# Holding back the fronts of the first six images, and image 0's second normalization in double steps

## The chip, the cores and the metric

The kernel runs on one core of a Trainium2 chip. The metric is the device time of one execution in microseconds (us). The kernel before was timed three times: the median is 1356.12 us, the lowest 1348.22 and the highest 1360.93.

## The reference

The input x has 32 images of 256 channels and 32 x 32 pixels in fp32. Two layers follow one another; each normalizes its input in groups of 8 channels (over all pixels of an image) and adds its result to what it got.

```python
x = x + conv3x3(quantize(gn(x)), quantize(w)) quantized, + bias          # layer 0
x = x + involution7x7(gn(x))                                             # layer 1

def involution(x):
    y = relu(bn(w1 @ x))                  # 256 -> 64 channels, per pixel
    w = w2 @ y + b2                       # 16 groups x 49 taps, per pixel
    out[c, p] = sum over taps of w[group(c), tap, p] * x[c, p + tap]
```

The quantization rounds to half precision. So layer 0 is an ordinary convolution whose weights are shared by all images. Layer 1 has weights of its own for every pixel, worked out from the normalized image, and every pixel's sum needs 49 of them for each of 16 groups.

## The kernel before, in words

**One image's path.** The generator `front(b)` (line 284) does what comes ahead of the window sums. Its statistics go over both halves of 128 channels: `add_up` (line 211) sums by a ScalarE activation with an accumulator, `group` (line 218) adds over 8 channels by two VectorE transposes and a reduction, `means`, `squares`, `variances`, `scales` and `finish` (lines 233 to 267) give 1/sigma (`rstd`) and the offset (`off`). `apply` (line 269) writes the normalized fp16 image `xq`. The convolution has four units (two halves of the pixels by two halves of the output channels). Each is 18 matmuls of 128x512 in two batches of nine (line 332); its PSUM result `pc` goes by way of `q` (line 346) back into x (line 348), and ScalarE sums x again (line 352). For image 0, every second unit uses another PSUM buffer, so two units can follow each other at once; else there is one buffer, and the next unit waits for `q`. Then the second normalization: mean, squares, variance, finish, and `xn` in two halves of channels, each with the left and the right side of the pixels (line 370). From `xn` come the features `py` and `y` (lines 377 and 388), and by transposes `pt` the `pixels` (lines 396 and 400).

**Weights and bands.** `weights(b, r0)` (line 403) makes `pw` from `y` with 32 small matmuls for four rows of pixels, eight times an image, and `evict` (line 435) writes them on VectorE into the ring `w_sb`. `scatter` (line 465) sends them by SP's queue to a DRAM buffer `wd`, seven transfers for each of four row blocks k of an image; `load_bands` (line 478) brings the block back as a band matrix, 14 transfers by POOL's queue and two by SP's. There are three band buffers. `sums` (line 510) multiplies band and pixels on TensorE into `acc`, `add_windows` (line 530) adds this to x, and `store` sends it out.

**The order.** It is written out by hand: the loop at line 556 counts a stage n, with 16 stages for each image. Every engine executes its instructions in exactly this order. Stages of image b, before: its front begins at n = 16b - 56 and takes some 50 stages, one step in each, so three or four fronts run at once; `weights` begins at 16b - 18, the sums at 16b. In every stage the fronts' steps come first, then the sums, then the weights. A front's steps, counted from its begin: statistics in steps 0 to 8, convolution from step 9 (a batch of nine matmuls in every second step) to 26, second normalization from 27 to 35, `py` at 36, transposes from 42.

```python
            later = list(fronts)
            for part in range(2):
                for b in list(later):
                    got = next(fronts[b], fronts)
```

A front that yields `LATER` goes on in the same stage, after the others have had their step.

Ahead of the first convolution VectorE writes the weights `wq` from a staging area that lies in two of the band buffers (`quantize_weights`, line 193); POOL clears these buffers and `w_sb` afterwards.

Of the kernel before, what the change touches and what calls it, by code (L numbers as in the profile page):

```python
# [9 lines left out]
F32 = mybir.dt.float32  # L10
AF = mybir.ActivationFunctionType
ALU = mybir.AluOpType

P = 128
B, C, H, W = 32, 256, 32, 32
N = H * W
NT = 512
RT = NT // W
CH = C // P
# [6 lines left out]
GN = 8  # L26
SQ = 32
GN_EPS = 1e-5
# [44 lines left out]
FRONT = -56  # L73
LOAD = -63
LEAD = 18


@with_exitstack
def tile_quant_conv_then_involution(
# [10 lines left out]
    nc = tc.nc  # L90
# [4 lines left out]
    small = ctx.enter_context(tc.tile_pool(name="small", bufs=2))  # L95
# [5 lines left out]
    ps_m = ctx.enter_context(tc.tile_pool(name="ps_m", bufs=1, space=PSUM))  # L101
# [40 lines left out]
    bands = [const.tile([P, SIDES, WINC * WB + PAD], F32, name=f"band_{i}") for i in range(NBAND)]  # L142
# [11 lines left out]
    wq = const.tile([P, CH, K0 * K0, C], F16, name="wq")  # L154
# [26 lines left out]
    for col, cols, at, n in (  # L181
# [4 lines left out]
        to = bass.AP(  # L186
            tensor=wd.tensor,
            offset=wd.offset + col * WPIX + at,
            ap=[[ROW, H], [WPIX, cols], [1, n]],
        )  # L190
        nc.sync.dma_start(to, bands[NBAND - 1][:H, 0, :n].unsqueeze(1).to_broadcast([H, cols, n]))

    def quantize_weights(kh):

        nc.vector.tensor_scalar(wq[:, kh], staged[kh], F16_MAX, -F16_MAX, ALU.min, ALU.max)
        nc.gpsimd.memset(bands[kh], 0.0)
        if kh == CH - 1:
            nc.gpsimd.memset(w_sb, 0.0)

    class GroupNorm:  # L200


        def __init__(self, b, layer):
            self.tiles = list(sums_sb[b % 2][layer])

        def begin(self, parts):
# [4 lines left out]
        def add_up(self, src, part, h, n0, n1, func, bias=0.0):  # L211
            junk = work.tile([P, N], F16, tag="junk", name="junk", bufs=1)
            i = part * CH + h
            nc.scalar.activation(  # L214
                junk[:, n0:n1], src[:, h, n0:n1], func, bias=bias, accum_out=self.sums[:, i : i + 1]
            )

        def group(self):


            if self.parts == 2:
                nc.vector.tensor_add(self.sums[:, :CH], self.sums[:, :CH], self.sums[:, CH : 2 * CH])
            across = small.tile([P, SQ], F32, tag="across", name="across")
            nc.vector.transpose(across, self.sums)  # L224
            total = small.tile([P, SQ // GN], F32, tag="total", name="total")
            nc.vector.tensor_reduce(
                total, across.rearrange("p (g r) -> p g r", r=GN), mybir.AxisListType.X, ALU.add
            )
            back = small.tile([P, SQ], F32, tag="back", name="back")
            nc.vector.transpose(back, total.unsqueeze(2).to_broadcast([P, SQ // GN, GN]))  # L230
            return back[:, :CH]
# [10 lines left out]
        def variances(self):  # L242
            pv = self.group()
            self.s = small.tile([P, CH], F32, tag="s", name="s")
            nc.scalar.activation(self.s, pv, AF.Sqrt, bias=eps, scale=1.0 / (GN * N))  # L245
            self.ve = small.tile([P, CH], F32, tag="ve", name="ve")
            nc.scalar.activation(self.ve, pv, AF.Identity, bias=eps, scale=1.0 / (GN * N))

        def scales(self):
# [3 lines left out]
        def finish(self):  # L253

            t = small.tile([P, CH], F32, tag="t", name="t")
            nc.scalar.activation(t, self.r, AF.Square)
            w = small.tile([P, CH], F32, tag="w", name="w")
            for h in range(CH):
                nc.scalar.mul(w[:, h : h + 1], t[:, h : h + 1], self.ve[:, h : h + 1])
            u = small.tile([P, CH], F32, tag="u", name="u")  # L260
            nc.scalar.activation(u, w, AF.Identity, bias=three_halves, scale=-0.5)
            self.rstd = small.tile([P, CH], F32, tag="rstd", name="rstd")
            self.off = small.tile([P, CH], F32, tag="off", name="off")
            for h in range(CH):
                one = slice(h, h + 1)
                nc.scalar.mul(self.rstd[:, one], u[:, one], self.r[:, one])
                nc.scalar.mul(self.off[:, one], self.m[:, one], self.rstd[:, one])
# [7 lines left out]
    LATER = 1  # L275

    def backwards(at):

        step, n = at.ap[-1]
        return bass.AP(tensor=at.tensor, offset=at.offset + step * (n - 1), ap=[*at.ap[:-1], [-step, n]])  # L280
# [3 lines left out]
    def front(b):  # L284


        xt = x_tiles[b]

        def stages(n):
            for _ in range(n):  # L290
                yield

        gn = GroupNorm(b, 0)
        gn.begin(1)
        for h in range(CH):
            gn.add_up(xt, 0, h, 0, N, AF.Identity)
            yield
        yield LATER
        gn.means()
# [12 lines left out]
        gn = GroupNorm(b, 1)  # L312
        gn.begin(N // NT)
        units = [(nt, mh) for nt in range(N // NT) for mh in range(CH)]
        for s in range(4 * len(units) + 2):
            u, i = divmod(s, 4)
            if u < len(units):
                nt, mh = units[u]
                if i == 0 and b == 0 and u % 2:

                    pc = ps_m.tile([P, NT], F32, tag="m", name="pc")
                elif i == 0:
                    pc = ps_c.tile([P, NT], F32, tag="pc", name="pc")
                for n in range(sum(CONV[:i]), sum(CONV[: i + 1])):
# [3 lines left out]
                    kh, k = n // (K0 * K0), (k + K0 * K0 // 2) % (K0 * K0)  # L328
# [7 lines left out]
                        start=n == 0,  # L336
                        stop=n == CH * K0 * K0 - 1,
# [28 lines left out]
        for h in range(CH):  # L366
            yield
            to = xn[:, h].rearrange("p (k d r j) -> p d k r j", d=SIDES, r=TR, j=JC)
            at = xt[:, h].rearrange("p (k r d j) -> p d k r j", d=SIDES, r=TR, j=JC)
            gn.apply(h, [(to[:, 0], at[:, 0]), (to[:, 1], backwards(at[:, 1]))])  # L370
        yield from stages(2)

        py = ps_m.tile([P, NT], F32, tag="m", name="py")
        for kh in range(CH):
            px = xn[:, kh].rearrange("p (a i n) -> p a i n", i=2, n=2 * JC)
            for i in range(2):
# [4 lines left out]
                    start=kh == 0,  # L381
                    stop=kh == CH - 1,
                )
        to = y_sb[b % 2].rearrange("p (k r d j) -> p d k r j", k=K, d=SIDES, j=JC)
        of = py.rearrange("p (k d r j) -> p d k r j", k=K, d=SIDES, j=JC)
        for d in range(SIDES):
            at = of[:, d]
# [3 lines left out]
        for m in range(0, M, 2):  # L391
# [7 lines left out]
            to = pixels[(b * M + m) // 2 % NPIX].rearrange("p i a (v c) -> p (i a) v c", c=GC)  # L399
# [130 lines left out]
    def add_windows(b, m):  # L530

        d = m % SIDES
        to = x_tiles[b].rearrange("p h (r c) -> p h r c", c=W)
        j0 = d * (JC - PAD1)
        for g, at, top, f, l in windows(b, m):
            x_at = to[:, :, f:l, j0 : j0 + WINI]
            of = at.rearrange("p h j r -> p h r j")[:, :, f - top : l - top]
            nc.vector.tensor_tensor(x_at, of, x_at, ALU.add)  # L538

    def store(b, k):  # L540

        cols = slice(k * NT, (k + 1) * NT)
        nc.sync.dma_start(out[b].rearrange("(h p) n -> p h n", p=P)[:, :, cols], x_tiles[b][:, :, cols])
# [3 lines left out]
    per = 2 * M  # L547

    def due(n, lag):

        b, i = divmod(n - lag, per)
        return (b, i) if 0 <= b < B else (None, None)

    with tc.manual_schedule():
        fronts = {}
        for n in range(FRONT, B * per + 2):
            b, i = due(n, FRONT)
            if i == 0:
                fronts[b] = front(b)
            later = list(fronts)  # L560
            for part in range(2):
                for b in list(later):
                    got = next(fronts[b], fronts)
                    if got is fronts:
                        fronts.pop(b)
                    if got is not LATER:
                        later.remove(b)
            if n in (FRONT + CH, FRONT + CH + 4):
                quantize_weights((n - FRONT - CH) // 4)
            b, i = due(n, 0)  # L570
            if b is not None and i % 2 == 0:
                sums(b, i // 2)
            b, i = due(n, 1)
            if b is not None and i % 2 == 0:
                add_windows(b, i // 2)
                if i // 2 == M - 1:
                    store(b, 1)
                    x_tiles.pop(b)

            b, i = due(n, 2)  # L580
            if b is not None and i == 2 * (M - 1 - SIDES):
                store(b, 0)
            b, i = due(n, -LEAD)
            if b is not None and i % 2 == 0:
                weights(b, i // 2 * WR)

            for part in range(2):
                b, i = due(n, -LEAD + 1 + part)
                if b is not None and i % 2 == 0:
                    for k in range(K):  # L590
                        if i // 2 == min((k + 1) * TR // WR, H // WR - 1):
                            scatter(b, k, part)
            b, i = due(n, LOAD)
            if i == 0 and b > 1:
                x_tiles[b] = load_x(b)

            b, i = due(n, 3 - 4 * NBAND)
            if b is not None and i % 4 == 0:
                load_bands(b, i // 4)
# [38 lines left out]
```

## Time and profile before

| | |
|---|---|
| median of three timed runs | 1356.12 us |
| the profiled execution | 1344.24 us |
| its span | 1342.5 us |
| TensorE busy | 1253.6 us (93%), mean granted clock 0.982 |
| VectorE, ScalarE, POOL busy | 61%, 55%, 76% |
| DMA | 361.85 MB, mean 270 GB/s |

The span is the time from the first to the last instruction of one execution under the hardware profiler; all starts in the timeline count from its begin. "Busy" counts the time in which an engine has an instruction at work. For TensorE the ends of the matmuls are modelled. In the answers PE is TensorE's matmuls, PEld its weight loads, DVE VectorE, ACT ScalarE; a name ending in q is an engine's queue as it issues transfers. A row of the timeline has its start and length in us, engine, line, operation, what it writes and reads, the shape, how many instructions it merges, and in brackets how long the engine had been idle and what released it. A row of the waits has the waiting engine and line, whom it waited for, the us in total, how often, and the longest.

### The profile page before, as it was taken

How to read it: one execution, taken by the hardware profiler on the slowest of the kernel's cores; microseconds unless marked ns; L12 is line 12 of the kernel's file. 1: busy time of each engine (PE TensorE's matmuls, PEld its weight loads, DVE VectorE, ACT ScalarE, POOL GpSimd, SP SyncE). 2: the span in 40 equal slices, each digit the busy share in tenths (PEclk: the TensorE clock that was granted, in tenths of full speed). 3: DMA queues.
4: the chain of work that ended last, by engine and by line, in shares of the span. 5: the costliest groups of instructions: out<-in, count | busy, mean ns of one | idle time of the engine just before them, and what ended most of it. 6: DMA issues, size and time to landing. Idle time of an engine off the chain costs nothing.

```text
span 1342.5 us, 65799 instructions
## 1 busy us (share of the span) xinstructions
PE 1253.6 (93%) x27648; PEld 763.7 (57%) x27648; DVE 818.8 (61%) x2539; ACT 733.3 (55%) x1731; POOL 1014.4 (76%) x1818
## 2 busy tenths in 40 slices
PE   5899999999999999999999999999999999999665
PEld 2356566565555655556655556666555566556454
DVE  3466666565666665656665666766666666666442
ACT  5775656455656556556545655655556564553300
POOL 9067878777787778777778787788777877788785
PEclk9999999999999999999999999999999999999987
DMA  6089999999999999999999999999999999999995
GB/s 228 11 237 295 271 293 293 279 266 281 272 286 282 291 285 270 283 263 280 293 282 283 270 288 282 293 297 296 281 288 275 277 284 290 271 281 266 278 274 166
DMA packets 360724, 361.85 MB, mean 270 GB/s; under 512 B 75056, under 2 KB 304752, under 8 KB 359152
## 3 DMA queue, kind: packets, MB, share of 16 engines
q1 hardware_dynamic: 278512, 229.38, 56.8%
q0 software_dynamic: 81920, 128.28, 33.9%
q8 instruction: 220, 3.60, 1.1%
q14 instruction: 72, 0.59, 0.1%
HBM read 176.60 MB, written 180.76 MB: 266 GB/s over the span
## 4 chain that ended last, share of the span: by engine, by line
PE 60%; DMA 23%; POOL 7%; issue 3%; ACT 3%; DVE 2%; SPq 1%; POOLq 0%; DVEq 0%; ACTq 0%
PE pc L332 25%; PE acc L522 19%; DMA band<-wd 17%; PE pw L411 11%; POOL band L497 7%; DMA wd<-w_sb 6%; PE pt L396 3%; PE py L377 3%; ACT junk L214 1%; SPq L476 1%; DVE w_sb L435 1%; DMA x<-in_x 1%; ACT xn L273 0%; SPq L497 0%; ACT xq L273 0%
## 5 line engine op out<-in xcount | busy, mean ns | idle before, releaser
L497 POOL DMA_DIRECT2D band<-wd x1792 | 980.3, 549 | 315.7 <-DMA band<-wd 182.0
L435 DVE TENSOR_TENSOR w_sb<-pw,late_sb 128x224 f32<-128x224 f32 (+7 forms) x1280 | 330.4, 322 | 419.5 <-PE pw L411 419.2
L332 PE MATMUL pc<-xq,wq 128*128 128x496 f16 (+3 forms) x2304 | 535.2, 379 | 20.3 <-ACT xq L273 18.3
L522 PE MATMUL acc<-band,pixels 64*32 64x190 f32 (+1 forms) x16384 | 426.6, 332 | 51.8 <-DMA band<-wd 42.7
L522 PEld LDWEIGHTS acc<-band,pixels 64*32 64x32 f32 x16384 | 304.7, 107 | 159.7 <-issue 81.1
L332 PEld LDWEIGHTS <-wq 128*128 128x128 f16 x2304 | 206.7, 98 | 316.1 <-issue 102.7
L411 PE MATMUL pw<-late_sb,y 64*32 64x224 f32 (+1 forms) x8192 | 288.9, 333 | 10.8 <-issue 9.4
L538 DVE TENSOR_TENSOR x<-acc,x 128x380 f32<-128x380 f32 (+1 forms) x512 | 262.0, 512 | 32.2 <-PE acc L522 23.2
L411 PEld LDWEIGHTS pw<-late_sb,y 64*32 64x32 f32 x8192 | 186.5, 106 | 38.1 <-issue 21.0
L400 ACT COPY pixels<-pt 128x512 f32<-128x512 f32 x128 | 73.7, 576 | 228.6 <-PE pt L396 228.6
L214 ACT ACTIVATE junk<-x 128x512 f16<-128x512 f32 (+1 forms) x192 | 146.4, 763 | 14.7 <-DVE x L348 12.2
L214 ACT ACTIVATE junk<-x,mean 128x1024 f16<-128x1024 f32 x128 | 147.1, 1149 | 4.3
L245 ACT ACTIVATE s<-back,eps 128x2 f32<-128x2 f32 x64 | 18.9, 296 | 178.6 <-DVE back L230 178.6
L346 DVE TENSOR_SCALAR q<-pc 128x512 f16<-128x512 f32 x128 | 87.2, 681 | 17.6 <-PE pc L332 17.6
L273 ACT ACTIVATE xn<-x,off,rstd 128x512 f32<-128x512 f32 x128 | 96.2, 800 | 0.0
L348 DVE SCALAR_TENSOR_TENSOR x<-q,early_sb,x 128x512 f32<-128x512 f16 x128 | 94.2, 736 | 0.3
L396 PEld LDWEIGHTS pt<-ident,xn 128*128 128x128 f32 x512 | 63.9, 142 | 26.3 <-issue 2.5
L396 PE MATMUL pt<-ident,xn 128*128 128x128 f32 x512 | 78.0, 275 | 0.1
L273 ACT ACTIVATE xq<-x,off,rstd 128x1024 f16<-128x1024 f32 x64 | 75.7, 1227 | 0.0
L235 ACT ACTIVATE mean<-back 128x2 f32<-128x2 f32 x64 | 12.6, 196 | 101.4 <-DVE back L230 101.4
L377 PE MATMUL py<-xn,early_sb 128*64 128x512 f32 x256 | 62.2, 606 | 0.9 <-ACT xn L273 0.9
L224 DVE STREAM_TRANSPOSE across<-sums 128x32 f32<-128x32 f32 x128 | 26.3, 205 | 33.6 <-ACT junk L214 32.4
(40 smaller groups left out, 369.3 us busy)
## 6 DMA issues: line engine op xcount, KB each, us to landing
wd<-w_sb SPq DMA_DIRECT2D x896, 160.0 KB
band<-wd POOLq DMA_DIRECT2D x1664, 70.5 KB, 4.6
x<-in_x SPq DMA_DIRECT2D x64, 512.0 KB
out<-x SPq DMA_DIRECT2D x64, 512.0 KB
band<-wd POOLq DMA_DIRECT2D x128, 60.5 KB, 4.6
band<-wd SPq DMA_DIRECT2D x128, 50.5 KB
band<-wd SPq DMA_DIRECT2D x128, 40.5 KB
band<-in_w SPq DMA_DIRECT2D x2, 1152.0 KB
```

Source lines behind the costliest of these rows:

```text
L214: nc.scalar.activation(junk[:, n0:n1], src[:, h, n0:n1], func, bias=bias, accum_out=self.sums[:, i : i + 1])
L273: nc.scalar.activation(dst, src, AF.Identity, bias=self.off[:, one], scale=self.rstd[:, one])
L332: nc.tensor.matmul(pc.rearrange("p (r c) -> p r c", c=W)[:, r0 - nt * RT : r1 - nt * RT, c0:c1], wq[:, kh, k, mh * P : (mh + 1) * P], xq[: ...
L346: nc.vector.tensor_scalar(q, pc, F16_MAX, -F16_MAX, ALU.min, ALU.max)
L348: nc.vector.scalar_tensor_tensor(xt[:, mh, cols], q, bias_sb[:, mh : mh + 1], xt[:, mh, cols], ALU.add, ALU.add)
L377: nc.tensor.matmul(py[i * CR : (i + 1) * CR], w1_sb[:, kh, :], px[:, :, i], start=kh == 0, stop=kh == CH - 1,)
L396: nc.tensor.transpose(pt[:, i, h * P : (h + 1) * P], xn[:, h, (m + i) * P : (m + i + 1) * P], ident)
L411: nc.tensor.matmul(pws[i][t * TW : (t + 1) * TW, : dj.stop - dj.start, r], y_sb[b % 2][half, (r0 // 2 + r) * W : (r0 // 2 + r + 1) * W], w ...
L435: nc.vector.tensor_tensor(to, of[:, :, d0:d1], bias[:, :, d0:d1], ALU.add)
L497: queue.dma_start(to, src)
L522: nc.tensor.matmul(at[t * TW : (t + 1) * TW, h, :, f - top : l - top], px[p, a, v * GC : v * GC + TW], of[:, :, a, f - top : l - top, v], ...
L538: nc.vector.tensor_tensor(x_at, of, x_at, ALU.add)
```

## The change

1. The fronts of images 0 to 5 are held back by 5, 5, 4, 3, 2 and 1 stages at their begin (`HELD`). They catch up later: in the last stages before their stage 37, as many as they were held, each takes two steps instead of one. So image 0 takes its steps 27 to 36, the second normalization and the features, in five double stages, while image 1, which has been held as long, is five steps less far than before in any stage until it catches up itself.
2. For image 0 the sum of the second half of channels goes to VectorE, the finish of both its normalizations to five VectorE operations, and one side of each half of `xn` to VectorE.
3. The clearing of the two staging buffers comes after both halves of `wq` are written, and the second half is written one stage later.
4. Ten matmuls on `wq` whose result nothing reads stand before the first convolution (`warm_up`).

```diff
+WARM = 10
+HELD = {0: 5, 1: 5, 2: 4, 3: 3, 4: 2, 5: 1}
+CATCH = 37
...
-        nc.gpsimd.memset(bands[kh], 0.0)
         if kh == CH - 1:
+            for t in bands[:CH]:
+                nc.gpsimd.memset(t, 0.0)
             nc.gpsimd.memset(w_sb, 0.0)
+    def warm_up():
+
+        pc = ps_m.tile([P, NT], F32, tag="m", name="warm_pc")
+        for _ in range(WARM):
+            nc.tensor.matmul(pc, wq[:, 0, 0, :P], wq[:, 0, 1:3], start=True, stop=True)
...
+        def add_up_by_vector(self, src, h):
+            nc.vector.tensor_reduce(self.sums[:, h : h + 1], src[:, h], mybir.AxisListType.X, ALU.add)
...
+            if self.first:
+                nc.vector.tensor_scalar(self.ve, pv, 1.0 / (GN * N), GN_EPS, ALU.mult, ALU.add)
+                return
...
+            if self.first:
+                self.rstd = small.tile([P, CH], F32, tag="rstd", name="rstd")
+                self.off = small.tile([P, CH], F32, tag="off", name="off")
+                nc.vector.tensor_mul(t, self.r, self.r)
+                nc.vector.tensor_mul(t, t, self.ve)
+                nc.vector.tensor_scalar(t, t, -0.5, 1.5, ALU.mult, ALU.add)
+                nc.vector.tensor_mul(self.rstd, t, self.r)
+                nc.vector.tensor_mul(self.off, self.m, self.rstd)
+                return
...
-            gn.add_up(xt, 0, h, 0, N, AF.Identity)
+            if b == 0 and h:
+                gn.add_up_by_vector(xt, h)
+            else:
+                gn.add_up(xt, 0, h, 0, N, AF.Identity)
...
-            gn.apply(h, [(to[:, 0], at[:, 0]), (to[:, 1], backwards(at[:, 1]))])
+            if b == 0:
+                one = slice(h, h + 1)
+                nc.vector.tensor_scalar(
+                    to[:, 0], at[:, 0], gn.rstd[:, one], gn.off[:, one], ALU.mult, ALU.add
+                )
+            else:
+                gn.apply(h, [(to[:, 0], at[:, 0])])
+            gn.apply(h, [(to[:, 1], backwards(at[:, 1]))])
...
-            later = list(fronts)
-            for part in range(2):
-                for b in list(later):
...
-            if n in (FRONT + CH, FRONT + CH + 4):
-                quantize_weights((n - FRONT - CH) // 4)
+            steps = [[b for b in fronts if not 0 <= n - FRONT - b * per < HELD.get(b, 0)]]
+            for b, held in HELD.items():
+                if CATCH - held <= n - FRONT - b * per < CATCH:
+                    steps.append([b])
+            for later in steps:
+                for part in range(2):
+                    for b in list(later):
+                        got = next(fronts[b], fronts)
...
+            if n == FRONT + HELD[0] + CH:
+                quantize_weights(0)
+                warm_up()
+            if n == FRONT + HELD[0] + CH + 5:
+                quantize_weights(1)
```

More of the change, by code (lines that the diff above doesn't have):

```diff
@@ L195, in quantize_weights @@
         nc.vector.tensor_scalar(wq[:, kh], staged[kh], F16_MAX, -F16_MAX, ALU.min, ALU.max)
-        nc.gpsimd.memset(bands[kh], 0.0)
         if kh == CH - 1:
+            for t in bands[:CH]:
+                nc.gpsimd.memset(t, 0.0)
             nc.gpsimd.memset(w_sb, 0.0)
+    def warm_up():
+        pc = ps_m.tile([P, NT], F32, tag="m", name="warm_pc")
+        for _ in range(WARM):
+            nc.tensor.matmul(pc, wq[:, 0, 0, :P], wq[:, 0, 1:3], start=True, stop=True)
     class GroupNorm:
         def __init__(self, b, layer):
+            self.first = b == 0
             self.tiles = list(sums_sb[b % 2][layer])
@@ L559, in tile_quant_conv_then_involution @@
                 fronts[b] = front(b)
-            later = list(fronts)
-            for part in range(2):
-                for b in list(later):
[L563 to L567, printed above, removed]
-            if n in (FRONT + CH, FRONT + CH + 4):
-                quantize_weights((n - FRONT - CH) // 4)
+            steps = [[b for b in fronts if not 0 <= n - FRONT - b * per < HELD.get(b, 0)]]
[6 more added lines that the diff above has]
+                        got = next(fronts[b], fronts)
+                        if got is fronts:
+                            fronts.pop(b)
+                        if got is not LATER:
+                            later.remove(b)
+            if n == FRONT + HELD[0] + CH:
[3 more added lines that the diff above has]
+                quantize_weights(1)
             b, i = due(n, 0)
```

## The prediction

> **What bounds the kernel now.** I read the page's totals first, then a table of stages, then the start in order of time, then the waits of the transfer queues.
>
> ```profile
> PE 1253.6 (93%) x27648; PEld 763.7 (57%) x27648; DVE 818.8 (61%) x2539; ACT 733.3 (55%) x1731; POOL 1014.4 (76%) x1818
> ...
> DMA  6089999999999999999999999999999999999995
> ```
>
> TensorE and the DMA engines are both near full from the third slice on. The stages (columns: stretch, its length, busy us of each engine with its instructions, granted clock, DMA share, GB/s):
>
> ```profile
> 0.00:35.00 35.00, 17.63 (x72) 7.66 (x73) 13.23 (x33) 21.31 (x50) 34.05 (x26) 1.00 0.59 219
> 35.00:55.00 20.00, 17.47 (x71) 6.83 (x70) 6.62 (x19) 16.36 (x37) 0.00 (x0) 0.91 0.01 2
> 55.00:88.00 33.00, 30.84 (x412) 14.66 (x420) 20.16 (x75) 25.92 (x67) 12.86 (x24) 1.00 0.58 144
> 88.00:235.00 147.00, 145.69 (x3286) 89.35 (x3274) 95.47 (x291) 88.33 (x206) 115.79 (x212) 1.00 0.98 287
> 235.00:1240.00 1005.00, 975.66 (x21936) 595.07 (x21927) 639.82 (x1999) 567.79 (x1345) 776.04 (x1420) 1.00 0.96 281
> ```
>
> Until 88 us TensorE loses 22 us and DMA lies still from 20 to 64 us. From 88 to 235 us both are full (TensorE 99%, DMA 0.98). From 235 us on TensorE loses another 29.3 us (1005 - 975.66): there DMA is late. The waits of POOL, which issues the band loads, say the same:
>
> ```profile
> POOL band L497 <- DMA band<-wd: 182.0, 237, 2.9
> POOL band L497 <- DMA wd<-w_sb: 63.2, 28, 37.1
> POOL band L497 <- PE acc L522: 3.0, 2, 2.8
> ```
>
> Once it has begun, POOL waits for earlier transfers, hardly for TensorE. So it counts when the stream of scatters and band loads begins, and whether TensorE keeps feeding it. The start, in order of time:
>
> ```profile
> 15.24 17.63 PE L332 MATMUL pc<-xq,wq 128*128 128x512 f16 x72 [15.24 <-ACT xq L273]
> ...
> 35.57 5.65 PE L332 MATMUL pc<-xq,wq 128*128 128x512 f16 x18 [2.71 <-ACT xq L273]
> ...
> 55.66 0.98 PE L411 MATMUL pw<-late_sb,y 64*32 64x224 f32 x32 [1.05 <-ACT y L388]
> ...
> 64.44 9.11 SPq L476 DMA_DIRECT2D wd<-w_sb  x11
> ...
> 71.74 5.60 POOL L497 DMA_DIRECT2D band<-wd  x10 [37.12 <-DMA wd<-w_sb]
> ...
> 80.51 1.08 PE L377 MATMUL py<-xn,early_sb 128*64 128x512 f32 x4 [0.90 <-ACT xn L273]
> ...
> 87.68 1.42 PE L522 MATMUL acc<-band,pixels 64*32 64x133 f32 x60
> ```
>
> First convolution at 15.24, first weights (pw) at 55.66, first scatter 64.44, first band load 71.74, image 1's features (py) at 80.51 after 0.9 us of stall, first window sums 87.68.
>
> [...] the first matmuls start 0.42 us apart until 19.8 us, later ones 0.22; after the 2.71 us gap a group of 18 takes 5.65 instead of 3.97 us. [...] SP's and POOL's transfers share the 16 engines; the trace has 0.96 to 0.98 in sum, so a late scatter is not made up by another queue.
>
> **Part by part.**
>
> *Statistics.* [...] But wq's first half, whose load lands at 8.4, holds VectorE from 8.46 to 10.28 as before, so the second group starts at 10.33 instead of 10.60: 0.3 gained (0 to 0.4). The finish is eight ScalarE operations (11.84 to 13.96) before; after, five small VectorE ones at 0.19 us (rows L116 to L178): xq can start near 12.6, not 13.96. The first xq (1.23) would let TensorE go at 13.85. wq's second half, moved behind the finish, ends by 14.5, needed by the tenth matmul at 16.6: nothing. The bands' memsets wait for it: POOL still ends with w_sb near 35 us, and the first write there is at 49: covered.
>
> *Warm-up.* Ten matmuls of 512 columns from 10.35 at 0.425 us end at 14.6 and lie in idle time, but delay the convolution from 13.85 to 14.65. It then runs at 0.22: 72 x 0.22 = 15.8, end 30.5 instead of 32.87: 2.4 us gained [...].
>
> *Image 1's first normalization.* Both images are held by five stages, so their order against each other stays: image 1's xq follows the second unit's end by the same 10.3 us, and TensorE gaps again (about 2.8 us, then cold). Its first unit starts near 33.3, ends at 39.0.
>
> *Image 0's second normalization.* Now only two units of image 1 stand before py(0), not three: one unit (3.97 + 0.78) leaves the way. Image 2's sums and squares (2.1 + 2.5 on ScalarE) no longer stand before y(0) except one sum of 1.2. Group at 39.8 (behind q of image 1's first unit), five VectorE operations until 42.9, then half of each xn on either engine, the last at 45.2, py until 46.2, y 47.35, half a unit of conv, first pw at 48.2: **7.5 us earlier** than 55.66.
>
> *What is paid for it.* Image 1 is now held by an odd number of stages: its q stands on VectorE behind the eviction of the pw just issued, and the next unit's matmul, in order behind that pw, waits for the one PSUM buffer. By the rows (pw to eviction 1.1, eviction 1.28, q 0.69) this is 1.7 us at its third unit and 2.2 before image 2's first. The third pw comes at 56.25 (before 62.31), the fifth at 65.4 (69.34), the seventh at 71.75 (75.61), so the scatters can start by 6.0, 3.9 and 3.9 us earlier.
>
> Then image 1's own short second norm. Its last conv ends at 59.7; mean behind the group (70.0), squares to 72.75, root, finish on ScalarE (2.2) to 77.0, xn halves with image 3's sum between to 81.1. TensorE, with four half units, four pw and two transposes, is at py(1) at 74.65: it stalls 3.9 + 1.65 = 5.5 us where before it was 0.9. Behind it stand the eighth pw (82.1, before 81.52) and the first sums (88.0, before 87.68), and two half units (4 us) are still owed. So TensorE is 4.3 us behind. Image 2 has nine stages at 2.3 us for a chain of 21 us: another 0 to 3; images 3 to 5 have 10 to 12: nothing. Say TensorE is 5.5 behind at image 5, and the DMA stream 4 ahead.
>
> *Which counts at the end.* SP's and POOL's own orders are unchanged, no transfer is added. After 235 us TensorE has 29.3 us of stalls into which a delay of 5.5 can vanish, while the DMA stream has next to none. I take the middle of the scatter shifts, -3.9: the profiled run's 1344.24 (1.74 around its span of 1342.5) becomes some 1340. That run is below all three timed runs; on their median, 1356.12 - 3.9 = **1352**. The ends of the unknowns: -6.0 - 3.9 (the holes in DMA between 65 and 90 us, from its shares 0.85, 0.60, 0.97, 0.85, 0.94, closed too) = -10; and +5.5 + 2.5.
>
> **Rivals.** *The whole head start counts* (0.25): DMA keeps 6 us and closes its holes: 1346, with luck 1340. For it: POOL's waits. Against: the eighth pw is not earlier. *TensorE sets the end* (0.20), the slower side: the stall of 5.5 us at py(1) and the owed half units reach the scatters of images 1 to 5, which SP issues as soon as w_sb is written (before, image 1's first at 96.59, its eviction ended at 96.1). A scatter that starts later than before takes the head start away; it decides once image 1's third pw is later than 93.5 by more than the transfers queued there. Then +5.5, 1361.6, up to 1364. For it: TensorE 99% busy from 88 to 235. *Nothing arrives* (0.10): transfers' own spread swallows the start: 1356. The forecast has 0.45.
>
> **Numbers.** The forecast's own range is 1346 to 1358; with the rivals and the spread of the three runs (-8 to +5 of the median) I give 1340 to 1363. Within 1% (13.6 us; about what a measurement of this kernel can tell from no change): 0.70; faster by more, mostly from the first rival, 0.20; slower by more, from the second, 0.10.
>
> **What would show it.** The first convolution near 14.7 with 0.22 us spacing; first pw near 48; first scatter near 58.5; a TensorE gap of several us on xn ahead of py(1) near 75 to 81; first sums near 88, not 80; less TensorE idle time between 235 and 1240 us. I am wrong if py(1) doesn't stall (then TensorE gains about 4 and the end 6 to 10), or if image 1's scatters start over 3 us later than 96.6.

## The result, and the profile after

The changed kernel takes 1388.24 us (median of four runs, 1383.53 to 1391.17), the kernel before beside it 1358.53 us (1348.22 to 1361.09). The ratio is 1.0249, with a 95% interval of 1.0205 to 1.0293: 2.5% slower, some 30 us more, well outside the range of the prediction. The profiled execution has a span of 1387.4 us. The profiled execution of before took 1344.24 us, 14 us less than the median of the runs beside the changed kernel, so the two traces differ by more than the medians do.

The stages of the changed kernel, in the columns of before (stretch, length, busy us by engine with instructions, granted clock, DMA share, GB/s):

```profile
0.00:35.00 35.00, 20.58 (x81) 8.62 (x82) 19.19 (x38) 15.73 (x32) 32.93 (x26) 0.95 0.58 219
35.00:55.00 20.00, 16.51 (x96) 6.37 (x94) 9.53 (x33) 14.73 (x31) 0.00 (x0) 0.91 0.01 2
55.00:88.00 33.00, 25.14 (x304) 11.21 (x304) 14.16 (x44) 21.25 (x51) 14.27 (x26) 0.91 0.61 161
88.00:235.00 147.00, 127.37 (x2556) 72.74 (x2555) 79.56 (x253) 73.75 (x171) 93.03 (x171) 0.95 0.81 228
235.00:1240.00 1005.00, 967.92 (x21704) 588.66 (x21704) 635.25 (x1985) 573.82 (x1359) 765.35 (x1400) 1.00 0.95 278
```

From 88 to 235 us, where both TensorE and DMA had been full, TensorE is now busy for 127.37 of 147 us (145.69 before), at a clock of 0.95, and DMA falls to 0.81. That is where most of the time went, in the stages of the held images. From the chain of features one reads the same: ScalarE writes the features y of image 0 at 50.30 us (54.61 before), of image 1 at 86.21 (83.61), of image 5 at 272.54 (234.32) and of image 31 at 1303.99 (1260.48). So 4 us won at image 0 are 38 us lost at image 5, and the loss stays.

The start of the changed kernel, in order of time (rows of TensorE, VectorE, POOL and SP):

```profile
11.02 3.74 PE L208 MATMUL warm_pc<-wq 128*128 128x512 f16 x10 [11.02 <-DVE wq L198]
...
12.96 5.99 POOL L201 MEMSET band<- 128x7056 f32 x1
...
13.34 6.82 DVE L198 TENSOR_SCALAR wq<-band 128x2304 f16<-128x2304 f32 x1
...
20.22 15.19 PE L361 MATMUL pc<-xq,wq 128*128 128x496 f16 x63 [3.41 <-DVE bn_ve L175]
...
52.19 0.97 PE L447 MATMUL pw<-late_sb,y 64*32 64x224 f32 x32
...
62.25 10.75 SPq L512 DMA_DIRECT2D wd<-w_sb  x11
...
69.57 7.86 POOL L533 DMA_DIRECT2D band<-wd  x14 [34.80 <-DMA wd<-w_sb]
...
81.75 1.60 PE L413 MATMUL py<-xn,early_sb 128*64 128x512 f32 x4 [3.43 <-ACT xn L299]
84.19 1.98 PE L413 MATMUL py<-xn,early_sb 128*64 128x512 f32 x4 [0.84 <-ACT xn L299]
...
93.28 1.40 PE L558 MATMUL acc<-band,pixels 64*32 64x133 f32 x60
```

The first convolution is cut in two: its tenth matmul waits until 20.22 for wq's second half, which takes VectorE 6.82 us. In the kernel before it took 1.80:

```profile
11.72 1.80 DVE L195 TENSOR_SCALAR wq<-band 128x2304 f16<-128x2304 f32 x1
```

The first pw comes 3.5 us earlier than before, not 7.5, and the first scatter 2.2 us earlier (62.25). py of image 1 stalls as foretold (3.43 + 0.84 us), and the first window sums start 5.6 us later than before (93.28). What TensorE waited for between 88 and 280 us, rows of its matmuls (us in total, times, longest), in the changed kernel:

```profile
PE pc L361 <- DVE q L375: 15.1, 9, 2.1
PE py L413 <- ACT xn L299: 6.1, 3, 3.8
PE pc L361 <- DVE sums L236: 1.5, 1, 1.5
```

The kernel before has no wait of a convolution on q in that stretch; its longest entry there is 1.7 us.

Why an odd hold makes a difference: the weights and their eviction are issued in even stages only, behind the fronts' steps of the stage. Without a hold, or with an even one, the q of a convolution unit falls in an even stage too, where it stands ahead of that stage's eviction. With an odd hold it falls in the next stage, behind the eviction.

One of the waits of the changed kernel close up, in image 3's convolution, VectorE and TensorE in order of time:

```profile
122.98 0.98 PE L447 MATMUL pw<-late_sb,y 64*32 64x224 f32 x32
124.07 1.28 DVE L471 TENSOR_TENSOR w_sb<-pw,late_sb 128x224 f32<-128x224 f32 x4 [0.86 <-PE pw L447]
125.27 0.68 DVE L375 TENSOR_SCALAR q<-pc 128x512 f16<-128x512 f32 x1
...
126.00 3.46 PE L361 MATMUL pc<-xq,wq 128*128 128x512 f16 x9 [2.05 <-DVE q L375]
```

The unit's last nine matmuls had ended by 121.7, but q stands behind the eviction of a pw that TensorE issued later. The next unit needs the one buffer that q empties, so TensorE waits for 2.05 us. In the nine matmuls behind this wait the granted clock is 0.58 (0.83 from 120 to 130 us), and they take 3.46 us instead of 2.08. In the kernel before, at a unit of its middle, it is the other way round, q (704.28) ahead of the pw and its eviction, and the next nine matmuls wait for nothing:

```profile
704.28 0.68 DVE L346 TENSOR_SCALAR q<-pc 128x512 f16<-128x512 f32 x1
...
705.72 1.22 PE L411 MATMUL pw<-late_sb,y 64*32 64x224 f32 x32
706.88 2.08 PE L332 MATMUL pc<-xq,wq 128*128 128x512 f16 x9
707.04 1.28 DVE L435 TENSOR_TENSOR w_sb<-pw,late_sb 128x224 f32<-128x224 f32 x4 [2.08 <-PE pw L411]
```

### The profile page after: what moved, and what is told of

The parts are those of the page before. It is cut to its first block, busy times and chain, and to the rows that moved or that the text cites. A ratio compares the mean times of both kernels' runs of the same rounds, so it can differ in the third digit from the quotient of the medians.

```text
span 1387.4 us, 65796 instructions
## 1 busy us (share of the span) xinstructions
PE 1265.3 (91%) x27658; PEld 762.0 (55%) x27658; DVE 828.6 (60%) x2554; ACT 729.7 (53%) x1709; POOL 1013.2 (73%) x1818
## 4 chain that ended last, share of the span: by engine, by line
PE 68%; DMA 16%; DVE 5%; POOL 4%; issue 3%; ACT 2%; SPq 1%; POOLq 0%; DVEq 0%
PE pc L361 28%; PE acc L558 21%; PE pw L447 13%; DMA band<-wd 10%; DMA wd<-w_sb 4%; POOL band L533 4%; PE py L413 3%; PE pt L432 3%; DVE w_sb L471 2%; SPq L512 1%; DMA out<-x 1%; ACT junk L225 1%; DVE q L375 1%; ACT xn L299 1%; DVE wq L198 1%
## 5 line engine op out<-in xcount | busy, mean ns | idle before, releaser
L225 ACT ACTIVATE junk<-x 128x1024 f16<-128x1024 f32 (+1 forms) x191 | 145.5, 762 | 19.5 <-DVE x L377 11.8
L413 PE MATMUL py<-xn,early_sb 128*64 128x512 f32 x256 | 64.7, 621 | 10.5 <-ACT xn L299 10.4
L249 ACT ACTIVATE mean<-back 128x2 f32<-128x2 f32 x64 | 12.6, 197 | 106.1 <-DVE back L244 106.1
L424 ACT ACTIVATE y<-py,bn_shift,bn_scale 128x256 f32<-128x256 f32 x64 | 32.4, 555 | 24.6 <-PE py L413 24.4
```

Source lines behind the costliest of these rows:

```text
L225: nc.scalar.activation(junk[:, n0:n1], src[:, h, n0:n1], func, bias=bias, accum_out=self.sums[:, i : i + 1])
L413: nc.tensor.matmul(py[i * CR : (i + 1) * CR], w1_sb[:, kh, :], px[:, :, i], start=kh == 0, stop=kh == CH - 1,)
```

## The experiments

Three theories: A, the hold by an odd number of stages puts q behind the eviction; B, the double steps leave the second normalization too little time, and TensorE waits for xn; C, the start up to the first sums. All results in one table (features y of images 0, 5 and 31 in the profiled execution, us; ratio to the kernel before with its 95% interval). The y come from one execution each, and the one of before was quick: at image 31 even two runs with a ratio below 1 come later than it. So the ratio counts.

```
                                      y(0)    y(5)    y(31)   ratio
before                                54.61  234.32  1260.48
changed                               50.30  272.54  1303.99  1.0249  1.0205 to 1.0293
even holds 4,4,4,2,2,0                52.47  250.97  1281.97  1.0122  1.0081 to 1.0162
no hold                               51.83  236.82  1265.24  1.0012  0.9982 to 1.0042
other order of clearing               46.72  266.00  1289.34  1.0210  1.0165 to 1.0254
hold only                             52.67  274.36  1306.54  1.0271  1.0209 to 1.0334
all images held by 1                  54.02  273.71  1505.81  1.1741  1.1674 to 1.1807
all images held by 2                  53.78  242.43  1272.62  0.9968  0.9940 to 0.9996
all images held by 4                  50.14  238.74  1300.66  1.0182  1.0125 to 1.0240
no hold, late clearing                48.07  234.77  1265.90  0.9934  0.9909 to 0.9958
late start                            64.42  250.46  1279.79  1.0053  1.0028 to 1.0077
all held by 1, later evictions        53.52  237.18  1263.56  1.0004  0.9977 to 1.0031
all held by 2, late clearing          47.43  236.83  1259.58  0.9922  0.9895 to 0.9950
changed, later evictions              49.35  244.82  1268.64  1.0035  1.0007 to 1.0063
```

**Even holds.** The changed kernel with

```diff
-HELD = {0: 5, 1: 5, 2: 4, 3: 3, 4: 2, 5: 1}
+HELD = {0: 4, 1: 4, 2: 4, 3: 2, 4: 2}
```

> The changed kernel with even holds only: images 0 to 5 held by 4, 4, 4, 2, 2, 0 stages instead of 5, 5, 4, 3, 2, 1. Theory A (an odd hold puts q behind the eviction of the pw just issued, so TensorE waits about 2.1 us at each new convolution unit of images 1, 3 and 5): between 88 us and image 5's features TensorE's waits on q (15.1 us as matmul, 14.9 as weight load) go to under 5 us, image 5's features come at 243 to 255 instead of 272.5 us, ratio to the kernel before 1.003 to 1.012. Theory B (the double steps leave too little time for the second normalization of images 1 to 5, and TensorE waits for xn): nearly as many double steps are left, image 5's features stay after 262 us, ratio 1.017 or more. Theory C (the start, up to the first sums, is what costs): no change, 1.022 or more.

Half of the loss is gone (1.0122, just above theory A's range), image 5's features come at 250.97, and the waits on q from 88 us until then are 1.8 us as matmul and 2.8 as weight load. Waits on xn stay at 6.2 us. Against B as the main cause, and against C, since here the first sums start at 92.48, nearly as late as in the changed kernel. What is left of the loss goes with these two, later first sums (4.8 us after those of before) and waits on xn; how it divides was not traced.

**No hold.** All of the change but the hold:

```diff
-HELD = {0: 5, 1: 5, 2: 4, 3: 3, 4: 2, 5: 1}
+HELD = {0: 0}
```

> The changed kernel without any hold and without double steps; VectorE statistics, warm-up and the later clearing of the staging buffers stay. Theories A and B: the order of images 1 to 31 is that of the kernel before, so image 5's features come within 6 us of 234 us and the ratio is 0.997 to 1.006; the 6.8 us of wq's second half (1.8 before) may leave 3 to 5 us of loss. Theory C: 1.02 or more.

1.0012: the parts for image 0 don't cost what was lost. Theory C falls as the main cause. (The first sums start at 85.37 here, so this run does not say what late first sums cost.)

**The hold alone,** on the kernel before: `HELD`, `CATCH` and the loop over `steps` of the change, with wq written five stages later because the front begins later; no warm-up, no VectorE statistics.

```diff
+HELD = {0: 5, 1: 5, 2: 4, 3: 3, 4: 2, 5: 1}
+CATCH = 37
...
-            if n in (FRONT + CH, FRONT + CH + 4):
-                quantize_weights((n - FRONT - CH) // 4)
+            if n in (FRONT + HELD[0] + CH, FRONT + HELD[0] + CH + 4):
+                quantize_weights((n - FRONT - HELD[0] - CH) // 4)
```

> The kernel before with the holds of 5, 5, 4, 3, 2, 1 stages and the double steps alone: no VectorE statistics, no warm-up, clearing as before. Theories A and B: the loss is here: ratio 1.018 to 1.028, image 5's features 28 us or more after those of the kernel before. Theory C: 0.99 to 1.006.

1.0271. The loss is the hold's.

**Other order of clearing.** In the changed kernel the two staging buffers are cleared in reverse order:

```diff
-            for t in bands[:CH]:
+            for t in bands[CH - 1 :: -1]:
                 nc.gpsimd.memset(t, 0.0)
```

> The changed kernel with the two staging buffers cleared in the other order, so that POOL's first long memset waits for wq's second half. If the 6.8 us of that VectorE operation come from the memset beside it, it takes 1.2 to 1.9 us, the first convolution isn't cut in two (TensorE gap of 3.4 us at 16.8 gone) and the first pw comes 4 to 6 us earlier than 52.2 us. Theories A and B: the rest of the loss stays, ratio 1.018 to 1.025. Theory C: ratio 1.00 to 1.012. If the memset is not the cause, the operation stays over 5 us.

wq's second half takes 1.35 us (6.82 in the changed kernel), the gap in the first convolution is gone, and the first pw comes at 48.61, 3.6 us earlier (a little less than expected, because now wq's first half takes 4.36 us, beside the pixels' memsets). The ratio hardly moves. So the 6.82 us of that VectorE operation go with the 5.99 us memset beside it, and they aren't the main loss.

**All images held by one, by two, by four stages,** on the kernel before with the hold's loop; if A is right, one stage for all 32 images must be far worse than two or four. The edit for one stage; for the others 2 and 4 stand in place of 1:

```diff
-HELD = {0: 5, 1: 5, 2: 4, 3: 3, 4: 2, 5: 1}
+HELD = {b: 1 for b in range(B)}
```

> The kernel before with all 32 images held by one stage (odd) and one double stage each; nothing else changed. Theory A (the odd hold): about 2.1 us at three to four unit starts an image, 6 to 9 us for each of 32 images: 190 us or more in all, of which DMA's own pace hides some 30: time above 1450 us, and TensorE waits on q all through. Theory B (too little time for the second normalization): one stage of it is lost, TensorE's waits on xn stay small: below 1370 us.

> The same with all 32 images held by two stages (even), two double stages each. Theory A: within 1% of the kernel before (1340 to 1365 us), no waits on q. Theory B: more than with one stage: two stages of the second normalization are lost in every image; slower than the run with one stage, by waits on xn.

> The same with all 32 images held by four stages (even), four double stages each. Theory A alone: still within 1% of the kernel before. Theory B as a second cause: with even holds of 4 the changed kernel's images 1 to 5 waited 6.2 us on xn in all, so some 2 to 4 us an image, 60 to 130 us over 32, less the 30 that DMA's pace hides: 1380 to 1460 us.

One stage: 1591.06 us. Two stages: 1351.11, a little quicker than the kernel before. Four: 1379.89, just below what B as a second cause gave (its 2 to 4 us of waits an image were too many: 45.2 us over 32 images as matmul, see below). Waits of TensorE in the whole execution with one stage:

```profile
PE pc L334 <- DVE q L348: 214.5, 121, 2.1
PEld L334 <- DVE q L348: 200.7, 90, 2.6
```

(matmuls and weight loads wait side by side: the two don't add up, the whole loss is 238 us) and with four stages:

```profile
PEld py L379 <- ACT xn L275: 89.7, 64, 2.9
PE py L379 <- ACT xn L275: 45.2, 62, 2.4
```

The 32 images have 128 convolution units; with the odd hold there are 121 waits for q. With four stages there is one, of 0.8 us, but nearly every py (two halves an image, 64) waits for xn; with two stages that is 3.2 us in four waits. So both causes exist: A costs some 7 us an image (238 us over 32), B with four stages under 1 us (27 us over 32), and with two nothing that can be measured.

**Later evictions.** The decisive one: the odd hold stays, and only the eviction moves. `weights` gives back its pw, and the eviction is issued one stage later, behind the front's steps:

```diff
+        return pws
+
+    def evictions(b, r0, pws):
+
...
+            b, i = due(n, -LEAD + 1)
+            if b is not None and i % 2 == 0:
+                evictions(*held_back)
             b, i = due(n, 0)
...
-                weights(b, i // 2 * WR)
+                held_back = (b, i // 2 * WR, weights(b, i // 2 * WR))
```

> The kernel before with all images held by one stage, as in the run that took 1591 us, but the evictions of pw moved by one stage: they stand behind the next stage's steps of the fronts, so in every image q stands ahead of them again. If the order of q and eviction on VectorE is the whole of the odd hold's cost: TensorE's waits on q fall from 214.5 + 200.7 us to under 30 each, and the time is 1340 to 1375 us. If something else of the odd hold costs (the batches of matmuls that fall together with pw, the transposes): over 1400 us.

1591 us become 1351.75 (ratio 1.0004), and of the convolution's waits on q only two are left, as many as in the kernel before (1.6 us too):

```profile
PE pc L334 <- DVE q L348: 1.6, 2, 0.8
```

The same in the changed kernel, with its holds of 5, 5, 4, 3, 2, 1:

> The changed kernel, holds of 5, 5, 4, 3, 2, 1 and all, with the evictions moved behind the next stage's front steps. If the order of q and eviction is the larger part of the loss: image 5's features come at 246 to 256 instead of 272.5 us, and the ratio is 1.004 to 1.014, as with even holds (1.0122). If not: 1.02 or more.

1.0035, and image 5's features at 244.82, both slightly better than expected. Of the 2.5% lost, 2.1 come back with the order of two instructions on VectorE. Image 5's features are still 10.5 us later than before, with 5.8 us of waits on xn.

**Does the start reach the end?** Once by starting earlier, once later. Earlier: the changed kernel without the hold, the staging buffers cleared in the other order and the pixels after them, all behind wq:

```diff
-    for t in pixels:
-        nc.gpsimd.memset(t, 0.0)
...
-            for t in bands[:CH]:
+            for t in [*bands[CH - 1 :: -1], *pixels]:
                 nc.gpsimd.memset(t, 0.0)
```

> The changed kernel without any hold, with the staging buffers cleared in the other order and the pixels cleared after them, so that no long memset of POOL runs beside wq's two VectorE operations. Both take 1.2 to 1.5 us each, the first convolution runs through from 13 to 14.7 us, the first pw comes at 48.5 to 50.5 us (53.7 without this edit), the first sums at 80 to 82.5 (85.4). If an earlier start reaches the end, ratio 0.993 to 0.998; if the transfers' pace sets the end whatever the start, 0.998 to 1.003.

```profile
10.13 4.45 PE L206 MATMUL warm_pc<-wq 128*128 128x512 f16 x10 [10.13 <-DVE wq L196]
14.38 15.60 PE L359 MATMUL pc<-xq,wq 128*128 128x512 f16 x72
...
49.96 0.97 PE L445 MATMUL pw<-late_sb,y 64*32 64x224 f32 x32
...
81.60 1.41 PE L556 MATMUL acc<-band,pixels 64*32 64x133 f32 x60
```

These are rows of its start: the warm-up runs into one unbroken convolution, the first pw is 5.7 us and the first sums 6.1 us earlier than before. The ratio is 0.9934, some 9 us (6 to 12) less than the kernel before. Later: the kernel before with a warm-up of 60 matmuls and nothing else,

```diff
+    def warm_up():
+        pc = ps_m.tile([P, NT], F32, tag="m", name="warm_pc")
+        for _ in range(60):
+            nc.tensor.matmul(pc, wq[:, 0, 0, :P], wq[:, 0, 1:3], start=True, stop=True)
...
+                if n == FRONT + CH:
+                    warm_up()
```

> The kernel before with 60 matmuls of 512 columns on wq's first half ahead of the first convolution and nothing else: ten cold (4.3 us) and 50 warm (10.8 us), from 10.35 to some 25.5 us. The first convolution starts about 10 us later but warm, so the first pw comes 7.5 to 8.5 us later, with every order unchanged. If the start passes to the end: ratio 1.004 to 1.008. If the spread of the transfers swallows it: 0.998 to 1.003.

The first pw comes at 65.47, 9.8 us later (more than expected; wq's first half was late too), and the ratio is 1.0053, some 7 us (4 to 10). So the start passes on in both directions; how much of it is less sure. The intervals allow one to one, but the run without a hold, whose first sums come 2.3 us earlier than before, shows no clear gain (1.0012, 0.9982 to 1.0042). The changed kernel's first sums are 5.6 us late, so a part of about that size in its 30 us may go by way of the start (not shown); with the later evictions they come at 86.53.

**The two gains together:** all images held by two stages, with the late clearing.

```diff
-HELD = {0: 0}
+HELD = {b: 2 for b in range(B)}
```

> The two edits that gained, together: all images held by two stages with two double stages each, and the changed kernel's parts for image 0 with the late clearing. If their gains (0.9934 and 0.9968) add: 0.987 to 0.992. If the pace of the transfers is the rest: 0.992 to 0.996. If the hold only shifts stalls: 0.995 to 1.000.

0.9922 is the best ratio of all, 1343.48 us; its interval overlaps that of the late clearing alone, so whether the hold by two adds anything stays open.

## Why the prediction was wrong

The step that failed is the price of the hold after image 1: "images 3 to 5 have 10 to 12: nothing. Say TensorE is 5.5 behind at image 5". I had the mechanism, named it for image 1 (1.7 us at its third unit, 2.2 us before image 2's first; the trace has 1.45 and 2.13), and then didn't carry it on: images 3 and 5 are held by 3 and 1, odd too, and for each of their units q stands behind an eviction. I priced for them only the room of the second normalization, and that too low: it cost 6.1 us of waits on xn in images 3 to 5, not nothing. TensorE was 38 us behind at image 5, not 5.5. Its columns from 88 us until image 5's features, before and changed:

```profile
88.00:234.32 146.32, 145.01 (x3253) 88.74 (x3242) 95.47 (x291) 87.65 (x205) 115.30 (x211) 1.00 0.98 288
88.00:272.54 184.54, 161.41 (x3322) 93.75 (x3328) 101.61 (x317) 95.59 (x221) 119.21 (x219) 0.96 0.83 231
```

It stands still for 23.1 us instead of 1.3. Of the nine waits on q (15.1 us), seven follow a q of images 3 and 5; the other two are 0.5 us each. The eighth such wait is put down to `sums`, a small operation right behind q. These eight, four for each image, are 15.5 us. At three of them the next nine matmuls took 3.4 to 3.6 us instead of 2.1: I had left the clock out as well, which at 0.96 instead of 1.00 over 184.5 us is some 7 us (an estimate). Another 3.7 us of idle time lie ahead of 88 us (25.8 instead of 22.1), and the rest is not traced.

The other steps, one by one:

- *Statistics, finish by VectorE*: right in direction, smaller in size. xq could start at 13.46 (13.96 before, 12.6 expected): wq's first half held VectorE until 10.96, not 10.28. VectorE's sum of the second half took 1.22 us (a sum on ScalarE 1.06 + 0.19), and each of its two sides of `xn` 0.54.
- *Warm-up*: right in size where the convolution is left whole (14.38 to 29.98 us in the run with the late clearing, so 72 matmuls in 15.60 us instead of 17.63; 14.65 to 30.5 expected).
- *Clearing*: "the bands' memsets wait for it ... covered" was wrong. The first buffer's memset needs only wq's first half, began at 12.96 and ended at 18.95; VectorE's second half, begun at 13.34, ended 1.21 us after it. It took 6.82 us beside that memset of 5.99, and 1.35 us in the runs with the other order of clearing and the late clearing, where no memset ran beside it; why it takes longer beside a memset, no trace shows. I had looked at the memset's deadline, not at what runs beside it.
- *First pw at 48.2*: 52.19, late by that memset; with the other order of clearing 48.61.
- *Stall at py of image 1*: right, 4.3 us (5.5 expected). Over all images the short normalization is a small cause: with even holds of 4 in all images it costs 1.8%.
- *Which counts at the end*: wrong. I let a delay of TensorE vanish in 29.3 us of later stalls, and a head start of the transfers count alone. But TensorE's idle time from 235 to 1240 us did not shrink, it grew to 37.1 us (1005 - 967.92), and of the late start of 9.8 us, 7 (4 to 10) arrived at the end. Image 1's first scatter came at 102.31 instead of 96.59, 5.7 us later, which I had named as a sign of being wrong. The trace of before pointed this way: TensorE stood still for only 1% between 88 and 235 us, so there was no room there for a loss.
- The rival "TensorE sets the end" had the right side and the right path (image 1's scatters come later), and 1361.6 us for 1388: the same term missed.

## What to carry to other kernels

In an order written out by hand, a shift by one stage changes more than time: two steps that never met may now meet on an engine that takes its work in the order written (here q, whose matmuls had ended by 121.7 us, began only at 125.27, behind the eviction). When a shift is priced, take every image with its own parity, and write down for each engine which of two instructions comes first. And an instruction that frees the only buffer of the fullest engine belongs ahead of all work that can wait; here the eviction moved behind it was worth 2% in the changed kernel and 15% with a hold of one stage in all images. On the kernel before, where the order is right, it was not tried.

## What the runs showed of the hardware

- The same VectorE operation, 128x2304 from fp32 to half precision, took 1.35 us alone, and 1.8, 4.4 or 6.8 us with POOL memsets beside it. The 6.82 us are beside one memset of 5.99 us that began 0.38 us earlier. The 4.36 us (first half, other order of clearing) are beside six short memsets, from 7.66 to 11.79: the operation ended at 13.0, 1.2 us behind the last of them. In the kernel before it ended at 10.28 (1.82 us), while they ran (7.65 to 14.20), and POOL's same six took 6.55 us instead of 4.13.
- Behind a gap of 2 us in TensorE's work the granted clock was sometimes lower and sometimes not: in the changed kernel seven convolution units up to image 5 waited 2.0 to 2.2 us for q. After three of them nine matmuls took 3.37 to 3.57 us (126.00, 140.54, 153.25) at a granted clock of 0.57 to 0.59, after the other four 2.06 to 2.08 at 1.00.
- Holding all images by two stages made the kernel 0.3% quicker (0.9940 to 0.9996), with no cause shown; with an interval that ends so close to 1 it may be chance.
